# Bias rows as single loads on two queues, and a group norm applied by another engine

## The chip, the cores and the metric

The kernel runs on one core of a Trainium2 chip. A core has a tensor engine (PE, with its weight load PEld), VectorE (DVE), ScalarE (ACT), GpSimd (POOL) and SyncE (SP), each with an instruction queue of its own that runs in order; 16 DMA engines move data between HBM and the on-chip memory (SBUF). The metric is the device time of one execution in microseconds; the lower the better.

## The reference

Eight images of 384 channels and 32 x 32 positions go through two layers. The first is an attention over the 1024 positions of an image, with a learned relative bias, on the group-normalised input; the second is another attention and a feed-forward part with sign weights. All of it is float32. Cut to what the change touches:

```python
def _relative_bias(h, w, mlp_w1, mlp_b1, mlp_w2, mlp_b2):
    coords = ...                                  # the 1024 positions
    rel = (coords[:, None, :] - coords[None, :, :]) / denom
    hidden = gelu(rel @ mlp_w1 + mlp_b1, approximate=False)
    return transpose(hidden @ mlp_w2 + mlp_b2, (2, 0, 1))   # 8 heads x 1024 x 1024

def _gn(v, G=32, eps=1e-5):                       # group norm over 12 channels x 1024
    g = v.reshape(B_, G, C_ // G, H_, W_)
    return ((g - mean(g)) / sqrt(var(g) + eps)).reshape(v.shape)

# layer 0
qkv = tokens(_gn(x)) @ qkv_w + qkv_b              # 8 heads of 48
attn = einsum('bhnd,bhmd->bhnm', q * scale, k) + _relative_bias(...)[None]
out = einsum('bhnm,bhmd->bhnd', softmax(attn), v)
x = x + (out @ proj_w + proj_b)
# layer 1: attention with 6 heads of 64, then a feed-forward part
```

The bias of a pair of positions depends on their difference alone, so it is a table of 63 x 63 = 3969 differences for each head.

## The kernel before

**Layer 0, per image.** The scores are worked out transposed, 128 keys on the partitions by 512 queries. An image is 32 *units* (pair of heads, half of the queries, quarter of the keys), in four pairs of eight units. A unit is 16 score matmuls into two PSUM tiles (`s`, line 688), two additions of the bias by VectorE (line 699, reading PSUM and `grow`), two exponentials by ScalarE (line 703) and 16 matmuls with `v` (line 719) that are issued two units later (`LAG = 2`). At a pair's second half the sums are inverted by GpSimd (line 748) and spread by DMA to `rb`, and GpSimd multiplies (line 760). PSUM holds four tiles of the kind, so the scores can't run far ahead of VectorE.

**The bias in SBUF.** `table` lies in HBM, one row of 3969 numbers per head. `grow` holds for each head 60 rows of 32 bias values on 128 partitions, in such an order that one addition can read a unit's bias as a plain stretch. It is filled in 32 parts (8 heads by 4 parts `c`). Each part is a *load* (`grow_load`, line 479) and a *turn* (`grow_turn`, line 491). The load brings 914 numbers of the table to each of 128 partitions, a different start on each: partition 32 dy + x begins 63 dy + x further on. Before, it is four loads, one for each `dy`, all issued by SP (line 486). The turn copies it backwards into `grow`, by ScalarE for even `c` (line 496) and by VectorE for odd `c` (line 498). The first 16 parts go through tiles `wide` of the pool `ep`; the last 16 (those "of the units") go through three places of `oT` that are free for so long (`staged` is 1, 2 or 3).

**The order around it.** The program order is written out by hand. `later` (class `_Later`) is a list of work with a number of steps; `later.step()` is called after each projection of the first image and after each unit, and does what has become due. So `later.after(i + 10, load)` puts the load of staged part i after 10 + i steps: six steps are the q and k projections, four the v projection, the rest the units. Lines 843 to 848 set the steps: part i of the last 16 is loaded at step i + 10 and turned at step i + 13 for i < 9, and at i + 12 after that. Between these, SP's queue also holds the transfers of the sums (lines 745 to 756), the parts of the weights that are stored as `cut` (line 122), `ready` (line 249) and the next image (`load`, line 343, at unit 12 of the first image). Each DMA carries one of eight counters in turn, and the program makes a DMA wait until the one that had the counter before has landed.

**The group norm of the next image** runs inside the units of the current one: `group_norm(b, xn)` (line 500) returns seven stages, three that measure (VectorE, line 513, and two small DMAs), one that works out mean and scale (GpSimd, lines 528 to 533, and two small DMAs) and three that apply it, one for each 128 channels. `apply` is VectorE's for image 0 (line 543) and ScalarE's for the others (line 547). The stages of image b + 1 are given out at unit 1 of image b (unit 12 for b = 0) with the steps (5, 6, 7, 10, 13, 14, 15), line 872. The normalised tile is read first by `ahead.mask` at units 28, 29 and 31 (lines 897 to 900).

Of the kernel before, what the change touches and what calls it, by code (L numbers as in the profile page):

```python
# [22 lines left out]
ALU = mybir.AluOpType  # L23
# [6 lines left out]
B, C, IH, IW = 8, 384, 32, 32  # L30
# [14 lines left out]
RW = 2 * IW - 1  # L45
NREL = RW * RW
QROWS = P // IW
# [227 lines left out]
def _layer0(tc, ins, x1, sums, shared, weights, beside):  # L275
# [4 lines left out]
    nc = tc.nc  # L280
# [4 lines left out]
    with ExitStack() as ctx:  # L285
# [8 lines left out]
        def etile(name, shape=(P, N), dtype=F32):  # L294
            return ep.tile(list(shape), dtype, tag="e", name=name)
# [4 lines left out]
        later = _Later()  # L300
# [25 lines left out]
        for g in range(P // QT):  # L326
            at = g * QN
# [10 lines left out]
        table = dram.tile([H0, NREL], F32, tag="table", name="table", bufs=1)  # L338
# [96 lines left out]
        WR = GW // 4  # L435
# [43 lines left out]
        def grow_load(h, c, staged):  # L479

            run = (WR - 1) * RW + IW
            wide = oT[:, staged, 0 : WR * RW] if staged else etile(f"wide{h}_{c}", (P, WR * RW))
            for dy in range(QROWS):
                src = table[h : h + 1, :]
                at = src.offset + NREL - 1 - (WR * (c + 1) + QROWS - 2 - dy) * RW - 2 * (IW - 1)
                nc.sync.dma_start(
                    wide[ts(dy, IW), 0:run], bass.AP(src.tensor, at, [[1, IW], [1, run]])
                )
            return wide

        def grow_turn(h, c, wide):
# [8 lines left out]
        def group_norm(b, xn):  # L500


            stats = small.tile([P, KC, NH, 6], F32, tag="gst", name=f"gst{b}")
            there = dram.tile([C, NH * 6], F32, tag="there", name=f"there{b}")
            back = dram.tile([C, 2], F32, tag="back", name=f"back{b}")
            gs = small.tile([GROUPS, C // GROUPS * NH, 6], F32, tag="gs", name=f"gs{b}")
            mv = small.tile([GROUPS, 2], F32, tag="gmv", name=f"gmv{b}")
            of = small.tile([GROUPS, C // GROUPS, 2], F32, tag="gof", name=f"gof{b}")
            sc = small.tile([P, KC, 2], F32, tag="gsc", name=f"gsc{b}")

            def measure(k):
                for h in range(NH):
                    nc.vector.bn_stats(stats[:, k, h, :], xn[:, k, ts(h, HALF)])

            def gather():
                with nc.allow_non_contiguous_dma(reason="statistics"):
                    nc.sync.dma_start(
                        there.rearrange("(k p) s -> p k s", p=P),
                        stats.rearrange("p k h s -> p k (h s)"),
                    )  # L520
                    nc.sync.dma_start(
                        gs.rearrange("g n s -> g (n s)"),
                        there.rearrange("(g r) s -> g (r s)", g=GROUPS),
                    )

            def scatter():
                nc.vector.bn_aggr(mv, gs)
                nc.gpsimd.tensor_scalar(mv[:, 1:2], mv[:, 1:2], 1e-5, 0.0, ALU.add, ALU.add)
                nc.gpsimd.tensor_tensor(mv[:, 1:2], mv[:, 1:2], rsqrt[:GROUPS], ALU.pow)
                nc.gpsimd.tensor_scalar(  # L530
                    mv[:, 0:1], mv[:, 0:1], mv[:, 1:2], -1.0, ALU.mult, ALU.mult
                )
                nc.gpsimd.tensor_copy(of, mv.unsqueeze(1).to_broadcast([GROUPS, C // GROUPS, 2]))
                with nc.allow_non_contiguous_dma(reason="statistics"):
                    nc.sync.dma_start(
                        back.rearrange("(g r) s -> g (r s)", g=GROUPS),
                        of.rearrange("g r s -> g (r s)"),
                    )
                    nc.sync.dma_start(sc, back.rearrange("(k p) s -> p k s", p=P))

            def apply(k):
                if b == 0:
                    nc.vector.tensor_scalar(
                        xn[:, k, :], xn[:, k, :], sc[:, k, 1:2], sc[:, k, 0:1], ALU.mult, ALU.add
                    )
                else:
                    nc.scalar.activation(
                        xn[:, k, :], xn[:, k, :], AF.Identity, scale=sc[:, k, 1:2],
                        bias=sc[:, k, 0:1],
                    )  # L550

            return [
                lambda: measure(0), lambda: measure(1), lambda: (measure(2), gather()), scatter,
                *(lambda k=k: apply(k) for k in range(KC)),
            ]

# [37 lines left out]
        def cut_tile(name):  # L594
            return etile(name)[:, 0 : 2 * C]
# [240 lines left out]
        def grow_turns(n):  # L836
            for _ in range(n):
                grow_turn(*waiting.pop(0))
# [4 lines left out]
            later.after(i + 4, lambda n=n: grow_turns(n))  # L843
            later.after(i + 2, lambda n=n: grow_loads(n))
        for i in range(len(parts) // 2):
            later.after(i + (13 if i < 9 else 12), lambda: grow_turns(1))
            at = 1 + i % NF0 if i < 12 else 2 + i % 2
            later.after(i + 10, lambda at=at: grow_loads(1, at))
        qk = project_qk(0, first)
# [2 lines left out]
        for k in range(KC):  # L852
            stages = _cut_weights(
                nc, k, plain[:, ts(k, 2 * C)],
                lambda name, k=k: (
                    spare if name == "ch" else plain[:, ts(k, 2 * C)] if name == "cl"
                    else cut_tile(f"{name}0{k}")
                ),
# [4 lines left out]
        for b in range(B):  # L863
            held = []
            for i, u in enumerate(units):
                done = held.pop(0) if len(held) == LAG else None
                held.append(
                    (u, scores(b, qk, u, lambda: weigh(b, *done) if done else None))
                )
                if i == (12 if b == 0 else 1) and b + 1 < B:  # L870
                    xn = load(b + 1)
                    for at, stage in zip((5, 6, 7, 10, 13, 14, 15), group_norm(b + 1, xn)):
                        later.after(at, stage)
                if i == 3 and b > 0:
                    project_out(b - 1, residuals(b - 1, etile), range(NF0))
                if b == B - 1:
                    for at, work in beside:
                        if at == i:
                            work()
                later.step()  # L880
                if i == 28 and b == 0:
                    cuts = _Cut(
                        nc, cut, BLOCKS,
                        shared.pool.tile([P, KC * 3 * C], F32R, tag="w", name="wc"),
                    )
                    for n in range(BB):
                        cuts.load(n)
                if b in (1, 2, 3) and i == 12:
                    t = cut_tile(f"cw{b}")
                    weights.load_part(b - 1, t)  # L890
                    for at, stage in enumerate(
                        weights.cut(
                            b - 1, t, lambda name, b=b, t=t: t if name == "cl" else cut_tile(f"{name}1{b}")
                        )
                    ):
                        later.after(4 + at, stage)
                if b + 1 < B and i in (28, 29, 31):
                    if i == 28:
                        ahead = Ahead(b + 1, xn)
                    ahead.mask((28, 29, 31).index(i))  # L900

            def weigh_held():
                finish = weigh(b, *held.pop(0))
                if finish is not None:
                    finish()

            if b + 1 == B:
                while held:
                    weigh_held()
                break  # L910
            order = [n % len(BLOCKS) for n in range(b % 2 * BB, b % 2 * BB + len(BLOCKS))]

            def project(some):
                for n in some:
                    ahead.project(cuts, n, (0, 1, 2) if n == order[0] else (2, 0, 1))
                    if n in order[:BB]:
                        cuts.load((n + BB) % len(BLOCKS))

            ahead.highs()
            for k in range(2):  # L920
                ahead.low(k)
            project_v(b + 1, xn, [0])
            weigh_held()
            ahead.low(2)
            weigh_held()
            ahead.mixed(0)
            project_v(b + 1, xn, [1])
            for k in range(1, KC):
                ahead.mixed(k)
            project(order[:BB])  # L930
            project_v(b + 1, xn, [2, 3])
            project(order[BB:])
            qk = ahead.qk
# [1352 lines left out]
```

## Time and profile before

| | us |
|---|---|
| device time, median of 3 runs | 2979.79 (2979.13 to 2980.34) |
| device time of the profiled execution | 2982.46 |
| its span, first to last instruction | 2980.7 |
| granted clock of the tensor engine, mean | 0.998 |
| first score matmul of image 0 / image 1 | 76.01 / 242.27 |
| turns of bias rows by VectorE (line 498), first to last | 44.4 to 144.3 |
| loads of bias rows (line 486), first to last issue | 36.4 to 139.3 |
| issue of one such load, SP, median | 0.419 |
| turn of one row by VectorE (line 498) / ScalarE (line 496) | 0.64 / 0.58 |
| group norm applied by ScalarE (line 547), 21 times, median | 1.229 |

The span is what the profile covers; the device time is longer than it by the little before the first and after the last instruction. Views of the profile give the busy time of each engine in a stretch, the waits with what ended them, and the instructions in order of time; times are from the start of the span. The DMA share is the mean busy share of the 16 DMA engines.

### The profile page before, as it was taken

To read this page: it belongs to the slowest core of one execution; us is meant where nothing else is said; L and a number is where in the kernel's file an instruction comes from. 1 tells how busy PE (TensorE), PEld (TensorE's weight loads), DVE (VectorE), ACT (ScalarE), POOL (GpSimd) and SP (SyncE) were. 2 spreads that over 40 slices of the span, in tenths; PEclk is the share of its full clock that TensorE was granted. 3 is DMA by queue.
4 is the path that set the end of the run, shared out by engine and by line. 5 is a ranking of instruction groups with operands and counts; after the bars stand their busy time and mean duration, and the time that the engine had idled before them with its cause. 6 is when DMAs were issued, how large, how long until landed. Compare 5 with 4: busy or idle time off the path is not lost.

```text
span 2980.7 us, 47053 instructions
## 1 busy us (share of the span) xinstructions
PE 2944.5 (99%) x19370; PEld 1658.2 (56%) x19370; DVE 1943.0 (65%) x1937; ACT 1525.3 (51%) x1864; POOL 468.4 (16%) x294
## 2 busy tenths in 40 slices
PE   8999999999999999999999999999999999999999
PEld 3345555555555655643545656746746747655553
DVE  3775748576675757564574785785775775775756
ACT  2553626354463636354373564564564564564644
POOL 2020201111010201102202202301302302302020
PEclk9999999999999999999999999999999999999999
DMA  7633131312203131222411111202202212112111
GB/s 196 170 91 93 45 111 38 94 47 65 78 16 111 24 97 31 53 98 60 108 70 26 48 62 54 90 24 68 85 17 77 75 31 71 67 40 82 40 45 38
DMA packets 129520, 203.71 MB, mean 68 GB/s; under 512 B 61872, under 2 KB 79648, under 8 KB 128816
## 3 DMA queue, kind: packets, MB, share of 16 engines
q1 hardware_dynamic: 126032, 198.77, 23.0%
q8 instruction: 156, 2.56, 0.4%
q10 hardware_dynamic: 3264, 1.82, 0.2%
q14 instruction: 68, 0.56, 0.1%
HBM read 152.99 MB, written 38.51 MB: 64 GB/s over the span
## 4 chain that ended last, share of the span: by engine, by line
PE 74%; DVE 3%; DMA 2%; ACT 2%; issue 1%; POOL 0%; SPq 0%; DVEq 0%; ACTq 0%
PE s L1638 11%; PE o L1687 10%; PE s L688 10%; PE o L719 9%; PE y2p L1932 6%; PE pg L170 5%; PE y1p L1881 5%; PE pv L1575 4%; PE pp L783 3%; PE pp L1784 3%; PE pm L170 3%; PE pv L662 3%; PE pq L1427 1%; DMA rb<-rd 1%; DVE qk L1508 1%
## 5 line engine op out<-in xcount | busy, mean ns | idle before, releaser
L703 ACT ACTIVATE e<-e 128x1024 f32<-128x1024 f32 x512 | 534.1, 1056 | 351.2 <-DVE e L699 334.8
L699 DVE TENSOR_TENSOR e<-s,grow 128x1024 f32<-128x1024 f32 x512 | 601.0, 1218 | 165.5 <-PE s L688 152.7
L688 PE MATMUL s<-qk 48*64 48x512 f32 x4096 | 614.9, 593 | 12.4 <-DVE e L699 12.1
L719 PE MATMUL o<-e,v 64*64 64x512 f32 x4096 | 608.3, 592 | 0.0
L1649 ACT ACTIVATE e<-s,kc 128x512 f32<-128x512 f32 x768 | 464.0, 694 | 172.9 <-PE s L1638 163.4
L1638 PE MATMUL s<-qk,qk 64*64 64x512 f32 x3072 | 418.9, 592 | 1.7 <-DVE oT L1697 1.5
L1687 PE MATMUL o<-e,v 64*64 64x512 f32 x3072 | 414.4, 590 | 0.0
L688 PEld LDWEIGHTS s<-qk 48*64 48x64 f32 x4096 | 229.6, 133 | 258.6 <-issue 120.0
L719 PEld LDWEIGHTS o<-e,v 64*64 64x64 f32 x4096 | 241.7, 133 | 202.1 <-issue 133.7
L1638 PEld LDWEIGHTS s<-qk,qk 64*64 64x64 f32 x3072 | 153.9, 132 | 192.0 <-issue 109.2
L1664 DVE TENSOR_TENSOR t<-t,e 128x1024 f32<-128x1024 f32 x192 | 230.9, 1221 | 45.5 <-ACT e L1649 45.4
L1687 PEld LDWEIGHTS o<-e,v 64*64 64x64 f32 x3072 | 159.8, 133 | 169.0 <-issue 141.9
L748 POOL TENSOR_TENSOR inv<-sums,over 128x16 f32<-128x16 f32 x32 | 95.8, 2994 | 888.0 <-DMA sums<-sd 552.9
L1868 DVE TENSOR_REDUCE parts<-y 128x1 f32<-128x1024 f32 x75 | 89.7, 1217 | 103.1 <-ACT y L1865 102.7
L1661 DVE TENSOR_TENSOR t<-e,e 128x1024 f32<-128x1024 f32 x96 | 114.1, 1223 | 59.4 <-ACT e L1649 59.4
L1544 POOL TENSOR_TENSOR hc<-hc,rsqrt 128x32 f32<-128x32 f32 x24 | 136.8, 5698 | 2.0
L662 PE MATMUL pv<-wv,xn 128*128 128x384 f32 x384 | 128.9, 490 | 0.0
L1575 PE MATMUL pv<-wv,bx 128*128 128x384 f32 x384 | 128.3, 491 | 0.0
L1784 PE MATMUL pp<-oT,L_attn_proj_wT 128*128 128x512 f32 x288 | 126.3, 595 | 1.9 <-DVE oT L1750 1.9
L783 PE MATMUL pp<-oT,wp 128*128 128x512 f32 x288 | 125.7, 595 | 0.0
L646 DVE SCALAR_TENSOR_TENSOR qk<-pg,qk 128x1024 f32<-128x1024 f32 x42 | 51.4, 1225 | 112.8 <-PE pg L170 98.1
L1575 PEld LDWEIGHTS pv<-wv,bx 128*128 128x128 f32 x384 | 119.4, 314 | 9.8 <-ACT e L1649 4.1
(212 smaller groups left out, 3513.2 us busy)
## 6 DMA issues: line engine op xcount, KB each, us to landing
rb<-rd SPq DMA_DIRECT2D x110, 256.0 KB
wc<-there SPq DMA_DIRECT2D x25, 576.0 KB
wc<-cut SPq DMA_DIRECT2D x24, 576.0 KB
xn<-in_x_dram SPq DMA_DIRECT2D x24, 512.0 KB
res<-in_x_dram SPq DMA_DIRECT2D x24, 512.0 KB
x<-res SPq DMA_DIRECT2D x24, 512.0 KB
bx<-x SPq DMA_DIRECT2D x8, 1536.0 KB
rq<-hi SPq DMA_DIRECT2D x48, 256.0 KB
```

What stands on the lines that cost most here:

```text
L170: self.nc.tensor.matmul(out[:, h], w[:, i, k], part[k][:, ts(h, HALF)], start=(k == 0 and i != 1), stop=(k == KC - 1 and i != 0),)
L662: nc.tensor.matmul(pv[:, i, 0:C], xn[:, k, ts(2 * m2 + i, P)], wv[:, k, :], start=(k == 0), stop=(k == KC - 1),)
L688: nc.tensor.matmul(s[j][ts(c, QP), i], qk[pair][rows, 1, ts(4 * m2 + 2 * i + c, QP)], qk[pair][rows, 0, ts(h, HALF)], start=True, stop=True,)
L699: nc.vector.tensor_add(e.rearrange("p (i q) -> p i q", i=2), s[j], bass.AP(near.tensor, near.offset, [near.ap[0], [-QROWS * IW, 2], [1, HA ...
L703: nc.scalar.activation(e, e, AF.Exp)
L719: nc.tensor.matmul(po[ts(j, S0), r], v[keys, 2 * m2 + i, 2 * pair + j, :], es[j][keys, ts(i, HALF)], start=(m2 == 0 and i == 0), stop=(m2 ...
L1575: nc.tensor.matmul(pv[:, i, 0:C], xt[:, k].rearrange("c (p m) -> c m p", m=MT)[:, 2 * m2 + i], wv[:, k], start=(k == 0), stop=(k == KC - 1),)
L1638: nc.tensor.matmul(s[j][ts(c, QP), i], qk[pair, 1][rows, ts(4 * m2 + 2 * i + c, QP)], qk[pair, 0][rows, ts(h, HALF)], start=True, stop=True,)
L1649: nc.scalar.activation(e[:, ts(i, HALF)], s[j][:, i], AF.Exp, scale=kc[:, pair, j, m : m + 1])
L1664: nc.vector.tensor_add(total[j], total[j], e)
L1687: nc.tensor.matmul(po[ts(j, D1), r], v[keys, 2 * m2 + i, at : at + D1], es[j][keys, ts(i, HALF)], start=(m2 == 0 and i == 0), stop=(m2 == ...
L1784: nc.tensor.matmul(pps[m][:, h], wp[:, k, ts(m, P)], oT[:, k, ts(h, HALF)], start=(k == 0), stop=(k == NP1 - 1),)
```

## The change

The four loads of a bias row become one, with a source of three dimensions: 4 steps of 63 numbers, 32 steps of 1, and 914 numbers. The rows of the last 16 parts are issued by ScalarE's queue instead of SP's. All of these are turned at step i + 12. The group norm of images 2 to 7 is applied by GpSimd, all three thirds at step 13; image 1 stays with ScalarE at steps 13, 14 and 15, and image 0 with VectorE.

```diff
             run = (WR - 1) * RW + IW
             wide = oT[:, staged, 0 : WR * RW] if staged else etile(f"wide{h}_{c}", (P, WR * RW))
-            for dy in range(QROWS):
-                src = table[h : h + 1, :]
-                at = src.offset + NREL - 1 - (WR * (c + 1) + QROWS - 2 - dy) * RW - 2 * (IW - 1)
-                nc.sync.dma_start(
-                    wide[ts(dy, IW), 0:run], bass.AP(src.tensor, at, [[1, IW], [1, run]])
-                )
+            src = table[h : h + 1, :]
+            at = src.offset + NREL - 1 - (WR * (c + 1) + QROWS - 2) * RW - 2 * (IW - 1)
+            (nc.scalar if staged else nc.sync).dma_start(
+                wide[:, 0:run], bass.AP(src.tensor, at, [[RW, QROWS], [1, IW], [1, run]])
+            )
             return wide
...
             def apply(k):
                 if b == 0:
                     nc.vector.tensor_scalar(
+                        xn[:, k, :], xn[:, k, :], sc[:, k, 1:2], sc[:, k, 0:1], ALU.mult, ALU.add
+                    )
+                elif b > 1:
+                    nc.gpsimd.tensor_scalar(
                         xn[:, k, :], xn[:, k, :], sc[:, k, 1:2], sc[:, k, 0:1], ALU.mult, ALU.add
                     )
                 else:
...
         for i in range(len(parts) // 2):
-            later.after(i + (13 if i < 9 else 12), lambda: grow_turns(1))
+            later.after(i + 12, lambda: grow_turns(1))
             at = 1 + i % NF0 if i < 12 else 2 + i % 2
             later.after(i + 10, lambda at=at: grow_loads(1, at))
...
                     xn = load(b + 1)
-                    for at, stage in zip((5, 6, 7, 10, 13, 14, 15), group_norm(b + 1, xn)):
+                    for at, stage in zip(
+                        (5, 6, 7, 10, 13, *((14, 15) if b == 0 else (13, 13))),
+                        group_norm(b + 1, xn),
+                    ):
                         later.after(at, stage)
```

The order of PE's instructions is the same before and after. VectorE's differs in where four of the turns stand, ScalarE's has 16 DMA issues more and 18 applies fewer, GpSimd's 18 applies more, SP's 112 issues fewer.

## The prediction

> **What bounds the kernel now.** I read the page first, then the busy time by stretches through the first image, then the waits of the tensor engine (PE) there, then the order in time around them.
>
> ```profile
> span 2980.7 us, 47053 instructions
> PE 2944.5 (99%) x19370; PEld 1658.2 (56%) x19370; DVE 1943.0 (65%) x1937; ACT 1525.3 (51%) x1864; POOL 468.4 (16%) x294
> DMA  7633131312203131222411111202202212112111
> ...
> core 0: us, PE busy (x) PEld busy (x) DVE busy (x) ACT busy (x) POOL busy (x), PEclk, DMA share, GB/s
> 24.00:76.00 52.00, 52.00 (x142) 24.33 (x141) 15.91 (x23) 7.67 (x11) 18.07 (x11) 1.00 0.92 220
> 76.00:80.00 4.00, 4.00 (x35) 1.39 (x34) 2.96 (x4) 0.68 (x1) 0.20 (x1) 1.00 0.83 342
> 76.00:110.00 34.00, 34.00 (x306) 15.16 (x309) 27.77 (x29) 22.61 (x25) 0.20 (x1) 1.00 0.66 186
> 110.00:150.00 40.00, 33.98 (x268) 11.70 (x264) 27.37 (x32) 20.35 (x24) 5.29 (x2) 0.87 0.56 158
> ...
> PE s L688 <- DVE e L699: 6.0, 2, 3.9
> ...
> 124.89 0.65 DVE L498 COPY grow<-oT 128x480 f32<-128x480 f32 x1 [4.82 <-DMA oT<-table]
> 137.33 0.65 DVE L498 COPY grow<-oT 128x480 f32<-128x480 f32 x1 [4.52 <-DMA oT<-table]
> 126.94 9.13 SPq L486 DMA_DIRECT2D oT<-table  x8
> ```
>
> PE is busy for 99% of the span, so only what makes PE wait, or takes such a wait away, moves the end. Two things matter here. In 24 to 110 us PE never waits, but the DMA engines are the busiest resource beside it (0.92 of 16 engines, 220 GB/s): this is the stage in which the bias rows are fetched. In 110 to 150 us PE loses 6.0 us to two stalls and runs at 0.87 of its clock. Both start where VectorE turns a bias row that hasn't landed (4.82 and 4.52 us); SP spent 9.13 us on two rows' eight loads. By the starts of the score matmuls a unit takes 3.44 us, but three units there took 10.11, 4.10 and 7.49: 21.70 - 3 x 3.44 = 11.4 us lost, 6.0 of it idle and the rest at the lower clock. That is all the first image can give.
>
> In images 2 to 7 a unit in the middle of an image takes 3.44 us, the three with the group norm's apply included; exceptions are the output projection and one unit of 4.09 us (22nd) in images 1 to 3, far from the apply:
>
> ```profile
> 477.75 1.23 ACT L547 ACTIVATE xn<-xn,gsc 128x1024 f32<-128x1024 f32 x1
> 480.77 1.23 ACT L547 ACTIVATE xn<-xn,gsc 128x1024 f32<-128x1024 f32 x1
> 483.86 1.23 ACT L547 ACTIVATE xn<-xn,gsc 128x1024 f32<-128x1024 f32 x1
> 470.00:480.00 10.00, 10.00 (x99) 6.20 (x95) 7.74 (x7) 6.97 (x9) 3.04 (x4) 1.00 0.38 93
> 480.00:490.00 10.00, 10.00 (x97) 6.22 (x93) 7.79 (x8) 8.14 (x9) 0.00 (x0) 1.00 0.14 41
> ```
>
> ScalarE has room for the three applies, and PE is busy 10.00 of 10.00 us beside them.
>
> **What the Trainium skill says.** "DMA: Bandwidth & Descriptors", section "Why a DMA increments its semaphore by 16 and not by 1": a DMA issued by SP or ScalarE runs on k of the 16 DMA engines, the largest k up to 16 that divides the count of the slowest dimension that isn't 1, of source and of destination. Its section "Rules for kernel authors" says that an outermost dimension of c < 16 confines the whole DMA to c engines. The trace agrees as far as it goes: a semaphore steps once for each engine and once for the rest, and I count nine steps for the stores of 8 table rows, three for the loads of 2 rows of rel, five for stores of 4 rows, sixteen for the bias loads of 32 rows. No load of before has a source and a destination that disagree. "SBUF — State Buffer", section "Door 1", says that partitions p and p + 32 share one DMA port; no view here separates that. "GPSIMD Engine Reference", section "Engine selection", has GpSimd roughly at line rate with one input.
>
> **The change part by part.**
>
> *One load per row.* A row was four loads, each 32 partitions by 914 elements; its source starts with a dimension of 32, so each ran on 16 engines. Now it is one load with a source of [4, 32, 914] against a destination of 128 partitions. By the page's rule k is the largest divisor of 4 and 128: 4. The bytes don't change, 128 x 3656 B = 468 KB a row, but 12 of 16 engines no longer carry any of it. Removed are 96 issues of 0.42 us (median of L486), which nobody waited for while rows came in time.
>
> Speed of an engine: 342 GB/s / (16 x 0.83) = 25.8 GB/s in 76 to 80 us, and 220 / (16 x 0.92) = 14.9 GB/s in 24 to 76 us, where the bias rows fill it. Four engines give 103 or 60 GB/s, a row takes 4.5 or 7.8 us. In the trace's DMA records a 3656 B piece takes 142 ns at its fastest and about 245 in that stage, which says the same. Which holds depends on whether the slowness in 24 to 76 us is that of 16 engines crowding on 32 partitions' ports (by the port page engines 0 and 1, then 2 and 3, would still crowd on one) or of the many at once. I take the middle in time, 6.2 us, and keep both ends.
>
> *First 16 rows, SP.* SP issues the first at 36.35 us; the first small load needed 2.4 us to land, of which I count 2 as fixed. They land one after another: 36.35 + 2 + 16 x 6.2 = 137.6 us. In VectorE's order the turn of the last one stands between the adds of unit 0 and of unit 1; it ran at 80.33 us. PE has at most two units' scores ahead, so it stops. Before that, VectorE turns rows 7, 9, 11 and 13 ahead of the v evictions, so PE already stops in the v projection.
>
> *Last 16 rows, ScalarE.* One is due per unit. While VectorE or ScalarE waits for row i, row i + 1 is already issued, so the four engines never run dry and a unit takes a row's time, not 3.44 us: 137.6 + 16 x 6.2 = 236.8 us. Other transfers that must pass the same four engines in that time: ready 1728 KB, xn 1536, rb 512, cut about 1300, the qk pieces 768, in all 5.85 MB; a sixteenth is 365 KB, at 25.8 GB/s 14 us. So the last row is there at about 251 us, where its turn was at 144.31: 107 us late. After it no stall differs from before. The 11.4 us are inside this: that last turn of before already came after the stalls.
>
> *ScalarE as issuer.* Sixteen issues of 0.29 (median of L329) to 0.46 us (L212) stand in the order ahead of the exponentials: 5 to 7 us, beside PE, since ScalarE is busy 22.61 of 34.00 us there. Each also waits for the transfer eight issues before it; by the program's order these are long landed (a row of three units before, the sum chain, the first half of rb). Nothing if rows come in time; and if they don't, the exponentials wait for the turn anyway.
>
> *Turns one unit sooner* for the first nine: VectorE and ScalarE wait for the row all the same; nothing more.
>
> *Group norm by GpSimd, six images.* 18 activations of 1.23 us leave ScalarE. On GpSimd 18 tensor_scalars of 128x1024 come; before shows none, the nearest being the two-input product of 2.42 us (L760) as the upper end and half of it as the lower. Three take 3.6 to 7.3 us. Behind them waits only the product oT x rb of that pair, and behind that the output projection, tens of us later; the normalised image is first read at unit 28, more than 40 us later. PE: 0. VectorE's adds read PSUM and one SBUF tile and didn't slow beside L760 (2.35 us for two at 130.45). Without that cover it would be one lost add, 1.2 us, per image.
>
> Sum on the profiled span: 2980.7 + 107 + 0 = 3088. The profiled execution took 2982.46 us, 2.67 over the median of 2979.79, so on the median: 2979.8 + 107 = 3087.
>
> **Rivals.**
> 1. *Four engines, no crowding:* 36.35 + 2 + 32 x 4.5 + 14 = 196 us, 52 late: 3032. For it speaks that 142 ns is the fastest piece at all times; against it, that no stage of bias rows ran near 25.8 GB/s an engine.
> 2. *Four engines, crowded:* 36.35 + 2 + 32 x 7.8 + 14 = 302 us, 158 late: 3138, some us more with PE at half clock after stalls. For it speaks that crowding lasted through 24 to 76 us.
> 3. *The other side, faster: the load is split over all 16 engines after all* (the instruction's shape taken apart differently, as by its 128 destination partitions). Then a row has one counter instead of four, SP no longer stands between rows behind rb and xn, a row lands 2 to 4 us after its issue with 5.8 us to go, and both stalls vanish: 2979.8 - 11.4 = 2968.4. It decides from k = 16 on; k = 8 would be 36.35 + 2 + 32 x 3.1 + 14 = 152, still 8 late. For it speaks only that no mismatched load is in this trace.
> 4. *16 engines, but ScalarE's waits give the gain back:* xn, rb and two rows ask for 3 MB in 10 us at about unit 13, 300 GB/s; one stall of some 4 us with its half clock returns, near 2979.
>
> **How the numbers follow.** Between the ends, 5 to 7.4 us a row (0.40), forecast 3087; near 4.5 us (0.20), near 7.8 or above (0.27); 16 engines and faster (0.11); given back (0.02). The sum over four engines is 0.87. Range 3020 to 3165: the lower end is rival 1 less the other transfers' 14 us, the upper is 8.6 us a row (54 GB/s): 36.35 + 2 + 32 x 8.6 + 14 = 327 us, 183 late, 3163. Left out are rivals 3 and 4 and some of the tails. A change of this kernel shows from about 0.2%, 6 us: slower 0.87, same 0.02, faster 0.11.
>
> **What would show it.** Right: the semaphore of a row's load steps five times; the DMA share falls to about a quarter in 40 to 200 us; large idle of VectorE and ScalarE at the turns, put down to the table's loads; a first score matmul well after 76 us and units of 5 to 8 us in image 0; images 1 to 7 with the same unit times, and no PE wait behind GpSimd's applies. Wrong: sixteen steps, and units of 3.44 us throughout.

## The result, and the profile after

The changed kernel takes 3050.91 us (median of 6 runs, 3047.36 to 3054.85) against 2980.03 us of the kernel before in the same session (2976.25 to 2982.39): ratio 1.0239, 95% interval 1.0226 to 1.0252, so 70.9 us slower. The forecast was 3087 us, in a range of 3020 to 3165.

First the page of the changed kernel. Of the clock and the DMA share each digit is a fortieth of the span, 76 us:

```profile
span 3053.1 us, 46878 instructions
PE 2964.9 (97%) x19370; PEld 1660.3 (54%) x19370; DVE 1943.4 (64%) x1937; ACT 1507.7 (49%) x1846; POOL 491.9 (16%) x312
...
PEclk9689999999999999999999999999999999999999
DMA  4334213131312203031331112211211211302111
```

The span grew by 72.4 us. Against the kernel before only the second and third digit of the clock (9 there) and the first four of the DMA share (7633 there) stand out: the loss is in the first image. PE's busy time rose by 20 us though it does the same work, since it runs slower around the stalls, as the granted clock in the next view shows. The same stretches as before, with the stretches that follow (columns as in the prediction):

```profile
24.00:76.00 52.00, 52.00 (x142) 24.33 (x140) 8.20 (x10) 4.91 (x6) 13.03 (x5) 1.00 0.42 129
76.00:110.00 34.00, 7.74 (x19) 1.43 (x18) 7.32 (x12) 2.37 (x4) 5.22 (x7) 0.54 0.34 114
110.00:150.00 40.00, 28.11 (x171) 9.52 (x175) 18.62 (x20) 14.50 (x17) 0.00 (x0) 0.71 0.33 127
150.00:200.00 50.00, 36.35 (x300) 13.80 (x292) 27.06 (x29) 22.72 (x26) 5.27 (x2) 0.92 0.45 137
200.00:250.00 50.00, 42.11 (x339) 14.54 (x343) 35.82 (x40) 25.14 (x27) 7.86 (x6) 0.88 0.26 73
250.00:300.00 50.00, 50.00 (x309) 27.92 (x302) 32.77 (x35) 22.87 (x24) 11.27 (x4) 1.00 0.40 111
```

Up to 76 us PE still has its projections to do, but VectorE did 10 operations where before it did 23, and the DMA share is 0.42 in place of 0.92: the rows move slowly while most of the DMA engines have nothing to do. Then PE runs out of work: 7.74 us of 34 are busy, at 0.54 of its clock. In 250 to 300 us it is busy throughout. The waits between 36 and 230 us say for what the engines stood (who waited, what ended it, us in total, times, the longest):

```profile
ACT grow L495 <- DMA wide<-table: 63.1, 7, 9.3
DVE grow L497 <- DMA wide<-table: 60.4, 8, 9.5
...
PE s L691 <- DVE v L670: 31.1, 4, 9.8
DVE grow L497 <- DMA oT<-table: 28.6, 7, 9.4
PE s L691 <- DVE e L702: 24.7, 9, 8.6
...
ACT grow L495 <- DMA oT<-table: 11.0, 6, 4.6
...
DVE e L702 <- DMA cut<-cd: 9.3, 1, 9.3
```

L495 and L497 are the turns (L496 and L498 before), L702 the additions of the bias, L670 the v evictions, with which VectorE takes the v projection out of PSUM. Nearly every turn now waits for its row, and PE waits for the evictions and additions that stand behind the turns: 31.1 and 24.7 us. The first score matmul starts at 86.02 us (76.01 before). The last turn of the first 16 rows ran at 122.28 us (80.33 before), the last of all at 213.92 us (144.31 before), 69.6 us late. Image 1 begins 71.6 us late, and the later images keep their times.

The trace's DMA records, counted out for this and for the kernel before (rows are counted from 0 to 31, the first 16 are 0 to 15):

| | before | after |
|---|---|---|
| semaphore steps of one row load | 16 (32 partitions) | 5 (128 partitions) |
| one 3656 B piece, median, while the first 16 rows load | 242 ns | 145 ns |
| a row's landing after the row before, rows 17 to 28, median | | 4.5 us |

### The profile page after: what moved, and what is told of

It reads as the page before. It is cut to its first block, busy times and chain, and to the rows that moved or that the text cites. A ratio compares the mean times of both kernels' runs of the same rounds, so it can differ in the third digit from the quotient of the medians.

```text
span 3053.1 us, 46878 instructions
## 1 busy us (share of the span) xinstructions
PE 2964.9 (97%) x19370; PEld 1660.3 (54%) x19370; DVE 1943.4 (64%) x1937; ACT 1507.7 (49%) x1846; POOL 491.9 (16%) x312
## 4 chain that ended last, share of the span: by engine, by line
PE 73%; DVE 3%; DMA 3%; ACT 1%; issue 1%; POOL 0%; SPq 0%; DVEq 0%; ACTq 0%; POOLq 0%
PE s L1644 10%; PE o L1693 10%; PE s L691 9%; PE o L722 9%; PE y2p L1938 5%; PE pg L170 5%; PE y1p L1887 5%; PE pv L1581 4%; PE pp L786 3%; PE pp L1790 3%; PE pv L665 3%; PE pm L170 3%; PE pq L1433 1%; DMA rb<-rd 1%; DVE qk L1514 1%
## 5 line engine op out<-in xcount | busy, mean ns | idle before, releaser
L702 DVE TENSOR_TENSOR e<-s,grow 128x1024 f32<-128x1024 f32 x512 | 601.1, 1218 | 172.6 <-PE s L691 152.2
L691 PE MATMUL s<-qk 48*64 48x512 f32 x4096 | 630.7, 603 | 61.9 <-DVE v L670 31.1
```

The costliest lines, as they stand in the source:

```text
L691: nc.tensor.matmul(s[j][ts(c, QP), i], qk[pair][rows, 1, ts(4 * m2 + 2 * i + c, QP)], qk[pair][rows, 0, ts(h, HALF)], start=True, stop=True,)
L702: nc.vector.tensor_add(e.rearrange("p (i q) -> p i q", i=2), s[j], bass.AP(near.tensor, near.offset, [near.ap[0], [-QROWS * IW, 2], [1, HA ...
```

## The experiments

Two questions had to be told apart: is it the number of DMA engines (theory A), or the issue from ScalarE, the single large load, the earlier turns or GpSimd? And how much does each half of the rows carry? The ratios are to the kernel before in the same session.

| run | us | ratio, 95% interval |
|---|---|---|
| e1, rows as two loads of 64 partitions | 3187.97 | 1.0702 (1.0685 to 1.0718) |
| e2, four loads again, all from SP | 2982.38 | 1.0008 (1.0002 to 1.0015) |
| e3, four loads, the last 16 rows' from ScalarE | 2980.99 | 1.0005 (0.9998 to 1.0012) |
| e4, one load, all from SP | 3055.56 | 1.0261 (1.0246 to 1.0277) |
| e5, before with the group norm on GpSimd | 2979.94 | 0.9996 (0.9988 to 1.0005) |
| e6, one load for the last 16 rows only | 3005.93 | 1.0082 (1.0066 to 1.0098) |
| e7, one load for the first 16 rows only | 3023.01 | 1.0137 (1.0121 to 1.0154) |
| e8, before with two moves in SP's order | 2971.60 | 0.9968 (0.9956 to 0.9981) |
| e9, after with the next image loaded later | 3044.87 | 1.0220 (1.0204 to 1.0237) |
| e10, the first move of e8 alone | 2977.14 | 0.9993 (0.9985 to 1.0002) |
| e11, the second move of e8 alone | 2976.72 | 0.9991 (0.9982 to 0.9999) |

**Is it the outermost dimension?** A row as two loads lies between one and four in number and size. By the rule of the prediction it is worse than either, because each of its sources starts with a dimension of 2.

```diff
-            (nc.scalar if staged else nc.sync).dma_start(
-                wide[:, 0:run], bass.AP(src.tensor, at, [[RW, QROWS], [1, IW], [1, run]])
-            )
+            for dy in range(0, QROWS, 2):
+                (nc.scalar if staged else nc.sync).dma_start(
+                    wide[dy * IW : (dy + 2) * IW, 0:run],
+                    bass.AP(src.tensor, at + dy * RW, [[RW, 2], [1, IW], [1, run]]),
+                )
```

> The changed kernel with each bias row as two loads of 64 partitions (source [2, 32, 914]) in place of one. Theory A (the outermost dimension of the source sets how many DMA engines carry a row): two engines, three semaphore steps a load, twice 4.5 us = about 9.1 us a row, the last of 32 rows at about 36 + 2 + 32 x 9.1 + 14 to 28 = 343 to 357 us, so 130 to 145 us later than in the changed kernel: 3180 to 3200 us. Rival (what costs is that a row is one large load that must land whole): two loads are nearer to the four of before, so between 2980 and 3051 us.

3187.97 us, and the trace has three semaphore steps for each load, turns in the second half that mostly follow one another after 8.9 to 9.1 us, and the last one at 349.6 us. Transfers that run on all 16 engines show the number too: the store of weights `cut<-cd` that was issued among the last rows of e1 has fourteen of its engines done within 2.7 us and two only after 11.7 us; in the changed kernel twelve are early and four late (below). Four of the turns in the order of time (start, length, then in brackets the idle time before and what ended it):

```profile
202.94 0.60 ACT L497 COPY grow<-oT 128x480 f32<-128x480 f32 x1 [4.86 <-DMA oT<-table]
211.99 0.65 DVE L499 COPY grow<-oT 128x480 f32<-128x480 f32 x1 [12.74 <-DMA oT<-table]
220.93 0.59 ACT L497 COPY grow<-oT 128x480 f32<-128x480 f32 x1 [4.93 <-DMA oT<-table]
229.89 0.65 DVE L499 COPY grow<-oT 128x480 f32<-128x480 f32 x1 [10.08 <-DMA oT<-table]
```

That falls in theory A's interval, and the rival is out: half of the engines make a row take twice the time, and neither the size nor the number of the loads sets it. A piece still takes 145 ns here, so the speed of one engine is the same whether two or four carry the rows.

The reverse puts back the four loads and keeps all else of the change:

```diff
-            (nc.scalar if staged else nc.sync).dma_start(
-                wide[:, 0:run], bass.AP(src.tensor, at, [[RW, QROWS], [1, IW], [1, run]])
-            )
+            for dy in range(QROWS):
+                src = table[h : h + 1, :]
+                at = src.offset + NREL - 1 - (WR * (c + 1) + QROWS - 2 - dy) * RW - 2 * (IW - 1)
+                nc.sync.dma_start(
+                    wide[ts(dy, IW), 0:run], bass.AP(src.tensor, at, [[1, IW], [1, run]])
+                )
```

> The changed kernel with the rows put back to four loads of 32 partitions each, all from SP; turns one unit sooner and the group norm on GpSimd stay. Theory A (the shape of the row loads is all the cost): 2975 to 2985 us, the same as before. Rival (the sooner turns or GpSimd's group norm cost part of the 71 us): over 2990 us, with waits of PE in images 2 to 7 or behind the turns of units 0 to 8.

2982.38 us, as theory A has it: with 16 engines a row, the rest of the change costs 0.02 to 0.15%, at most 4.5 us. One trace of it holds a small loss that the changed kernel covers up: the fifth unit of image 0 takes 4.97 us in place of 3.44, with a third wait of VectorE for a row (in 76 to 200 us 11.3 us in three waits, 9.3 in two before), so a turn one unit sooner can come before its row.

**Is it ScalarE's queue?** The diff of e3 is that of e2 with `(nc.scalar if staged else nc.sync)` kept as the issuer; e4 is the changed kernel with `nc.sync` for every single load.

> The changed kernel with the rows as four loads each, those of the last 16 rows issued by ScalarE. It asks what ScalarE costs as issuer when the loads run on 16 engines. Theory A (issues beside PE's work): 64 issues of 0.3 to 0.5 us are 19 to 32 us over 17 units, 1.1 to 1.9 us a unit on an engine that is busy about two thirds: 2980 to 3000 us. Rival (ScalarE's queue is the cost of the change: its waits hold back the exponentials): over 3020 us even with 16 engines.

> The changed kernel with all 32 single loads issued by SP. Theory A (four engines set the time whoever issues): 3040 to 3065 us, units of image 0 as long as in the changed kernel. Rival (ScalarE as issuer is part of the 71 us): under 3030 us, since the exponentials no longer stand behind issues and their waits; if SP in turn holds the rows behind the loads of the next image, the last three rows come later and it is over 3065 us.

e3 takes 2980.99 us: 64 issues on ScalarE, where the change puts 16, cost at most 0.12% by the interval. e4 takes 3055.56 us; its first units are about as long as the changed kernel's (18.84 and 12.97 us against 18.92 and 12.58). So who issues is not the cause. Of the last rows the trace of e4 shows the turns late by up to 14.83 us and the last at 216.6 us, since SP has stores and loads that wait for others ahead of them; but the 4.7 us that e4 has over the changed kernel is no more than the two intervals leave open.

**Which rows?** In e6 and e7 a row is one load in one half and four loads from SP in the other:

```diff
+            single() if staged else four()
```

(e7: `four() if staged else single()`; the two bodies are those of the changed kernel and of the kernel before.)

> The changed kernel with single loads for the last 16 rows only (from ScalarE); the first 16 are four loads each from SP. Theory A (four engines, 4.5 us a row, the last three held up by about 17 us by the other transfers on the same engines): the last row's turn at 76 + 2 + 16 x 4.5 + 17 = 167 us in place of 144, 20 to 25 us: 3000 to 3006 us. Rival (the last 16 rows, one due in each unit of 3.44 us, are the main cost, as each unit lost more than its row): over 3030 us.

> The changed kernel with single loads for the first 16 rows only; the last 16 are four loads each from SP. Theory A: the first unit's turns are 42 us late as in the changed kernel, the rows after them come at the full rate, and the stalls of before (11 us) are gone or stay: 2980 + 42 - 11 to + 42 = 3011 to 3022 us. Rival (the first 16 rows cost little, since the v projection has other work to do): under 3000 us.

e6 is 24.8 us slower, within theory A's interval, and e7 41.9 us, 1 us beyond it. In e6 the turns of the last rows end at 171.2 us, where 167 was expected. The waits of PE between 36 and 400 us tell the two halves apart, first those of e6, then those of e7:

```profile
PE s L702 <- DVE e L713: 27.6, 9, 8.8
```

```profile
PE s L702 <- DVE v L681: 30.3, 4, 8.7
...
PE s L702 <- DVE e L713: 6.3, 3, 3.1
PE o L733 <- DVE e L713: 5.1, 1, 5.1
```

In e7 PE waits for the v evictions (L681 here), which stand on VectorE behind the turns of the first rows, and the small stalls of the kernel before are still there; in e6 PE waits for the adds, which stand behind the turns of the last rows. The sum of both, 66.6 us, is near the change's 70.9.

**Is it GpSimd?** e5 is the kernel before with the group norm's part of the diff alone.

> The kernel of before with only the group norm's apply of images 2 to 7 moved from ScalarE to GpSimd. Theory A (hidden beside PE): 2980 us within 3 us; three applies of about 1.2 us each on GpSimd and no wait of PE behind them. Rival (an add of VectorE or the product oT x rb is held up): 1 to 4 us for each of six images, 2986 to 3004 us.

2979.94 us, no change. In the changed kernel three applies take 3.56 us on GpSimd (a window of one image), and in that stretch PE is busy 4.00 of 4.00 us:

```profile
544.28 3.56 POOL L546 TENSOR_SCALAR xn<-xn,gsc 128x1024 f32<-128x1024 f32 x3 [3.51 <-DMA gsc<-back]
547.80 2.41 POOL L763 TENSOR_TENSOR oT<-oT,rb 128x1024 f32<-128x1024 f32 x1
```

```profile
544.00:548.00 4.00, 4.00 (x43) 2.46 (x39) 3.66 (x4) 2.47 (x3) 3.72 (x4) 1.00 0.80 229
```

**Why are the last three rows later still?** In the changed kernel row 28 lands at 185.5 us, row 31 only at 211.8: 26.3 us for three rows. In the order of time around them:

```profile
184.54 0.51 ACTq L485 DMA_DIRECT2D oT<-table  x1
185.75 1.63 SPq L343 DMA_DIRECT2D xn<-in_x_dram  x3
187.48 0.69 SPq L122 DMA_DIRECT2D cut<-cd  x1
...
198.99 0.65 DVE L497 COPY grow<-oT 128x480 f32<-128x480 f32 x1 [9.39 <-DMA oT<-table]
...
206.67 0.59 ACT L495 COPY grow<-oT 128x480 f32<-128x480 f32 x1 [3.68 <-DMA oT<-table]
211.65 2.36 DVE L702 TENSOR_TENSOR e<-s,grow 128x1024 f32<-128x1024 f32 x2 [9.28 <-DMA cut<-cd]
213.92 0.64 DVE L497 COPY grow<-oT 128x480 f32<-128x480 f32 x1
```

The next image's load and the weights' store (`cut<-cd`) are issued between the rows. By the DMA records twelve of the store's 16 engines are done 10.0 to 10.5 us after its issue, and the other four only after 23.4 to 24.07 us, at 211.55 us: there VectorE stood 9.28 us behind the store, and not behind a row. e9 gives the next image's load out three units later (and its stages 1 to 2 units closer, so that they keep their place):

```diff
-                if i == (12 if b == 0 else 1) and b + 1 < B:
+                if i == (15 if b == 0 else 1) and b + 1 < B:
...
-                        (5, 6, 7, 10, 13, *((14, 15) if b == 0 else (13, 13))),
+                        (4, 5, 6, 8, 11, 12, 13) if b == 0 else (5, 6, 7, 10, 13, 13, 13),
```

> The changed kernel with the first image's load of the next image given out three units later. Theory A (rows 29 to 31 come late because the 1.5 MB of the next image pass the same four DMA engines first): those rows come every 4.5 us again, row 31's turn at 201 us in place of 213.9: 3036 to 3042 us. Rival (it is the reciprocal sums' store and the projection weights, or the place on the queue): 3048 to 3055 us, with row 31 still turned near 214 us.

3044.87 us, between the two: the last turn is at 209.2 us, 4.7 us earlier, where 13 had been expected, and the intervals of both ratios overlap. But the edit hardly moved the load in time. In both kernels SP reaches it only after the loads of `rb`, which wait for the store of the reciprocal sums to land (at 184.4 us, and in e9 at 183.5):

```profile
185.42 8.20 SPq L343 DMA_DIRECT2D xn<-in_x_dram  x3
```

The first of the load's three transfers is issued at 185.42 us, where the changed kernel has 185.75, and the other two, at 192.1 and 193.3, some 6 us later than there. What did change is the order: the store of weights goes ahead of the load, and its last engine is done at 201.4 us, where the add behind it starts. Rows 29 to 31 still share the time with the load and take 24.7 us. So e9 doesn't tell whether the load, the store or the loads of `rb` hold these rows; that stays open, as no run has the load start after row 31.

**A version that beats both.** The prediction had named the two stalls of the kernel before, 11.4 us. e8 leaves its loads as they are and changes SP's order in image 0: the store of the reciprocal sums, for whose data from GpSimd SP stood still for 4.3 us, two units later, and the next image's load three units later (with the stages of its group norm 1 to 2 units closer, as in e9).

```profile
SPq L749 <- POOL inv L748: 4.3, 1, 4.3
```

```diff
-                nc.sync.dma_start(rd.rearrange("j (p c) -> (j p) c", c=2 * N // P), inv)
-
+
+            def store():
+                with nc.allow_non_contiguous_dma(reason="sums"):
+                    nc.sync.dma_start(rd.rearrange("j (p c) -> (j p) c", c=2 * N // P), inv)
+
+            if b == 0:
+                later.after(2, store)
+            else:
+                store()
...
-                if i == (12 if b == 0 else 1) and b + 1 < B:
+                if i == (15 if b == 0 else 1) and b + 1 < B:
                     xn = load(b + 1)
-                    for at, stage in zip((5, 6, 7, 10, 13, 14, 15), group_norm(b + 1, xn)):
+                    for at, stage in zip(
+                        (4, 5, 6, 8, 11, 12, 13) if b == 0 else (5, 6, 7, 10, 13, 14, 15),
+                        group_norm(b + 1, xn),
+                    ):
```

e10 makes the first of the two moves alone and e11 the second with its stages; their expectations, the second and third below, were written when e8's time was known.

> The kernel of before with its four loads a row, and in the first image alone the store of the reciprocal sums given to SP two units later and the next image's load three units later. Theory A (the two stalls of before in 120 to 145 us come from rows whose loads stand behind these on SP's in-order queue): the stalls go, up to 11.4 us: 2968 to 2976 us. Rival (the rows are late for want of DMA engines, not for their place in the queue): 2978 to 2985 us, with the stalls still there.

> The kernel of before with only the store of the reciprocal sums given to SP two units later in the first image. Theory A (SP stands behind this store while GpSimd's power is out, and the rows behind it are late): the larger part of the 9.6 us that both moves together gave, 2972 to 2976 us. Rival (the next image's load is what holds the rows): 2978 to 2982 us.

> The kernel of before with only the next image's load given out three units later in the first image. Theory A (the store of the reciprocal sums is what holds SP): 2976 to 2982 us. Rival (1.5 MB of the next image ahead of the rows on the queue and the engines are what makes them late): 2970 to 2974 us.

e8 takes 2971.60 us, 9.6 us less (0.9968, 0.9956 to 0.9981). SP's order in the kernel before, then in e8:

```profile
116.34 0.34 SPq L749 DMA_DIRECT2D rd<-inv  x1
116.77 1.77 SPq L486 DMA_DIRECT2D oT<-table  x4
...
125.12 1.71 SPq L343 DMA_DIRECT2D xn<-in_x_dram  x3
126.94 9.13 SPq L486 DMA_DIRECT2D oT<-table  x8
```

```profile
111.13 1.76 SPq L486 DMA_DIRECT2D oT<-table  x4
...
115.92 0.37 SPq L752 DMA_DIRECT2D rd<-inv  x1
...
129.04 1.70 SPq L486 DMA_DIRECT2D oT<-table  x4
130.84 1.32 SPq L343 DMA_DIRECT2D xn<-in_x_dram  x3
```

A row that stood behind the store until 116.77 us is issued at 111.13, and the eight issues that took SP 9.13 us behind the next image's load come ahead of it. PE's waits for the adds in 76 to 200 us fall from 6.5 to 1.2 us. In the one trace of each, either move alone takes one of the two stalls away: in e10 the unit of 10.11 us is gone and that of 7.49 has become 10.80, in e11 the first is 10.03 and the second gone. The second varies between executions, though: in the trace of e5, whose first image is that of the kernel before, the two units took 10.54 and 4.41 us. The medians of e10 and e11 are 2.6 and 3.0 us below the kernel before; e10's interval holds 1, e11's ends just under it. So e10 fell between what its two theories expected, and e11 at the edge of theory A's; the store was not the larger part of it, and by the medians the two causes weigh about the same. Together they give 9.6 us and singly 5.6 in sum, but the intervals (5.7 to 13 us together, up to 4.5 and 5.4 singly) don't show that one move needs the other.

## Why the prediction was right, and which term was off

That the change makes the kernel slower was foreseen, and by the mechanism that the runs show, but the loss was put at 107 us and 71 came. The range of 3020 to 3165 us was wide enough for that; a row took 4.9 us on average, just below the 5 to 7.4 of the main case and near the 4.5 of rival 1, which had been given half its chance.

- *Four engines.* Right, and by the reason given. The Trainium skill, "DMA: Bandwidth & Descriptors", section "Why a DMA increments its semaphore by 16 and not by 1", gives k = 4 for [4, 32, 914] against 128 partitions; the trace has five steps for a row, and e1 three with an outermost dimension of 2. e2 shows that this is the whole cost within 0.15%. The two rivals that expected 16 engines are out.
- *A unit takes a row's time.* Right on average: units 6 to 15 of image 0 (from 0) take 4.46 us in the mean, and units 4 to 13 in e1 9.19. The signs named beforehand had two details wrong: the units alternate, 3.44 us and then up to 6.9, in place of 5 to 8 us each, and the DMA share was 0.33 to 0.45 and not a quarter, since other transfers run beside the rows.
- *A row's time.* This term was mis-sized: 6.2 us was taken, as the middle of 4.5 and 7.8. The measured times are (122.28 - 38.35) / 16 = 5.25 us a row in the first half, start included, and 4.5 us in the second. The upper end rested on the slowness of the kernel before, 242 ns a piece, as if it could belong to the rows' partitions; with four engines, and with two, a piece takes 144 to 145 ns. The crowding that rival 2 and the forecast's middle carried on did not appear. Over 32 rows that is 198.4 us forecast and 156 measured, 42.4 too many.
- *Other transfers on the same engines.* Forecast 14 us. Measured in the second half: 91.6 us from the last turn of the first half to the last turn of all, less 16 x 4.5 = 19.6 us, 5.6 more. This is a remainder and not one cause: by the landings, 4.1 us of it lie at row 16, which comes while `ready` is stored, 12.8 at rows 29 to 31, and 2.1 between the last row's landing and its turn, as VectorE stood behind the store of weights. That rival 1, which had the right row time, came out at 3032 and not at 3051 is due to this and to the first half's 5.25 us. What the term had not seen is the other direction: the rows also hold up what shares their four engines, as that store.
- *Nothing after the last row.* The two corrections bring the sum to the 69.6 us of the last turn by construction, since the second is the remainder. What can be checked is the rest: 69.6 us at the last turn, 71.6 at the start of image 1 and 70.9 between the medians, so nearly all of the loss has been made by then.
- *ScalarE as issuer costs nothing.* Right by e3 and e4, as far as their intervals go. The issues took 0.51 to 0.62 us each, more than the 0.29 to 0.46 assumed.
- *Turns one unit sooner.* Not tried alone; in the traces of e2 and e3 one early unit each is 1.5 us longer.
- *Group norm on GpSimd.* Right: 1.19 us each, the lower end of the bound, and no effect on PE (e5).
- *The 11.4 us of the first image.* Named as all that it could give; e8 has 9.6 of them, by another way than the change's.

## What to carry to other kernels

Fewer issues are no gain when the merged load starts with a short dimension: write down the outermost dimension of both sides first, since it and not the byte count or the number of partitions set the time here (16 engines, four, two: +3, +71, +208 us). When a resource is slow under full load, don't carry its slow speed over to a case in which a quarter of it works; here the fastest single piece of the kernel before, 142 ns, was close to what four engines then took, 144 ns, and its median of 242 ns was not. And on an in-order queue look for the issue that waits for another engine's result just ahead of the loads that are needed next.

## What was not expected of the hardware

- One DMA engine moves a 3656 B piece in 144 to 145 ns with two or four engines busy, and in 242 ns in the median with 16 (3656 / 144 = 25.4 GB/s, and 15.1). Which shared resource makes the difference was not tried; the crowding of few engines that the prediction had weighed shows in no trace here.
- A transfer over 16 engines ends with its slowest, and a few engines with other work are enough. In the trace of the changed kernel the first of the three loads of the next image had twelve engines done after 6.3 to 7.0 us and four after 12.0 to 12.3; the weights' store ended after 24.1 us, and the same kind of store later in the image, with no rows beside it, after 2.8 to 2.9 us. An add of VectorE then waits for the store, though by this split of the engines it is the rows that held the store up.
